# A fused slot-attention and FFN kernel: other places for an output block's mixed product, for low-part scalings and for queue steps

## The chip, the cores and the metric

The kernel runs as one program on one core of a Trainium2 chip. The metric is the time of one execution on the device, in microseconds (us). Each kernel is run several times and the median is given. One further execution is taken by the hardware profiler; its page and its trace are what this document reads. The engines are named as the profile names them: PE is TensorE's matrix products, PEld its weight loads, DVE is VectorE, ACT is ScalarE, POOL is GpSimd, SP is SyncE, which here only issues DMAs.

## The reference

The input is four token blocks of 512 tokens with 512 features (`hidden_states`, B = 4, T = D = 512). A layer norm without weights comes first, then an attention with gated slots, added to the input; then a second layer norm and a small FFN, added again.

```
q, k, v, s = split into 16 heads of xn @ Wq, @ Wk, @ Wv, @ Ws     # q, k: 64, v: 128, s: 64 slots
s = clip(s, -32, 32)
z = cumlogsumexp(s over t);  g_t = exp(z_{t-1} - z_t);  p_t = exp(s_t - z_t)
hk = hk * g_t + k_t p_t^T ;  ok_t = q_t hk          # first pass over the 64 slots
pv = softmax(ok)
hv = hv * g_t + p_t v_t^T ;  o_t = pv_t hv          # second pass
o  = o * rsqrt(mean(o^2) + eps) * g_norm * silu(xn @ Wg)
x  = x + o @ Wo
x  = x + (silu(xn2 @ fp8(gate_w) * scale) * (xn2 @ fp8(up_w) * scale)) @ fp8(down_w) * scale
```

All of it is in float32 from the outside. The recurrences over tokens are computed block by block.

## The kernel before, in words

Work is cut into 32 units. A unit is one group `g` of two heads (8 groups) for one token batch `b`. The units run in pairs of batches: for batches 0 and 1 the groups 0 to 7, each for both batches, in the order (0,0), (0,1), (1,0), (1,1), ... (7,1); then batches 2 and 3 in the same way. A unit is written (g,b). `first_unit` is (0,0), and `attention` (the function with most of the calls that the diff touches) writes all others. Unit (0,0) has no predecessor; every other unit also finishes the unit before it, which is called `before` in the code: it scales, transposes, splits and projects that unit's output while its own projections run. The last unit's output is finished inside the FFN.

A float32 product is made from three products of a shorter float type (`fp32r`): an operand is split into a high part, a low part and a part `less` that mixes both. The main product takes two passes (8 matmuls of 512 columns for a projection of the tokens), the mixed product one pass (4 matmuls). ACT copies the main product from PSUM with a factor, DVE then subtracts the mixed product. In `project_output` (L842) the inner dimension is only two heads, so the main product `p` has 4 matmuls and the mixed product `m` has 2. There are four such blocks `n` in a unit, one for each 128 tokens: p0, m0, p1, m1, p2, m2, p3, m3. ACT's copy `y` is L860, DVE's subtraction is L865 (`add_output`), and L866 adds the block to the residual stream in device memory by a DMA of POOL.

PSUM has three pools. `ps3` with tag `proj` has 3 buffers; all projections and both products of `project_output` rotate in it. `ps2` with tag `acc` has 2 buffers (the scores `a` and the outputs `ov`). `ps1` has three single banks that `bank()` hands out in turn: for transposes, for the states between blocks, and for the masked products `b`. A buffer is given again only when the last reader of its former content is done.

In order, a unit does: the slot scores `s`, keys `k`, queries `q` (each main and mixed), transposes of e and k; in even groups the values `v` of four token blocks (for two groups together); the transposes of the former unit's output (`turn_output`), its high part (`high_output`, ACT), low part and `less` (`split_output`, DVE, L832 to L836) and the scaling of the low part (`low_output`, ACT, L840); the products q times k with the mask; the gate `g` (`gate_main` twice and `gate_mixed`, copies on ACT at L519, main products at L514 and mixed ones at L537); the read of the slots (`ok`, `okn`), the softmax; then the output blocks 0 to 3, between them the transposes of the weights `w`; then `weight_slot`: the products `b` (L604), masked on DVE (L608); then `read_out`: the output `ov` by L765 and L774. The products at L774 wait for the masks.

The order on every engine is written by hand: the program has no scheduler (`tc.manual_schedule`). What goes on beside the units is held in two lists. `steps` holds the transposes of a coming layer norm; `next_step()` takes one. `work` holds small pieces on ACT, DVE, SP and POOL: scaling and splitting of weights (in `load_matrix`: `high` on ACT at L255, `rest` on DVE at L262 and L267, then a fetch and, at the end, a store of the split weights by SP), parts of layer norms (`measure`, `normalise` at L347, `parts` at L369 and L371, `scale_low` on ACT), and, for batches 2 and 3, the rounding of the FFN's weights to fp8 (DVE work and load and store DMAs; three steps make one piece). `other()` takes `pace[0]` entries of `work`, `other(1)` one, `piece()` takes entries up to the first that does not end a name with "_", `need(name)` takes all up to a name. `small` is `other` or `piece`, by the unit. `load(name)` issues the DMA of a coming matrix. `turned()` is true while parts of a layer norm stand first in the queue: this is so around the turn to the next pair of batches and to the FFN, in (7,0), (7,1), (0,2), (7,2) and (7,3), and at the start.

Of the kernel before, what the change touches and what calls it, by code (L numbers as in the profile page):

```python
# [37 lines left out]
F32 = mybir.dt.float32  # L38
# [6 lines left out]
P = 128  # L45
# [4 lines left out]
def kernel(  # L50
# [20 lines left out]
    B, T, D = x.shape  # L71
# [22 lines left out]
    ps3 = ctx.enter_context(tc.tile_pool(name="ps3", bufs=3, space=bass.MemoryType.PSUM))  # L94
# [15 lines left out]
    def bank(name, n=None):  # L110
        if n is None:
            n = turn[0]
            turn[0] = (n + 1) % 3
        if n in held:
            held.pop(n)()
        return ps1.tile([P, 512], F32, tag=f"bank{n}", name=name)
# [46 lines left out]
    work = []  # L163

    pace = [1]

    def other(count=None):
        for _ in range(count or pace[0]):
            if work:
                work.pop(0)[1]()  # L170

    def piece():

        while work:
            name, run = work.pop(0)
            run()
            if not name.endswith("_"):
                break

    def need(key):  # L180

        while any(name == key for name, _ in work):
            other(1)
# [4 lines left out]
    for g in range(NG):  # L188
# [3 lines left out]
        for nm in names:  # L192
            n = g if nm != "v" else 0 if g == 0 else (g + 1) // 2
# [94 lines left out]
    def turned():  # L288

        return bool(work) and work[0][0][:3] == "xs_"  # L290

    def next_step():
        if steps:
            steps.pop(0)()
# [340 lines left out]
    class Heads:  # L635
# [203 lines left out]
            lo = self.oT[:, 1, h, :]  # L839
            nc.scalar.mul(lo, lo.bitcast(F32), 1.0 / DELTA)  # L840

        def project_output(self, n):  # L842

            name = f"ps_o_{self.u}_{n}"
            p = ps3.tile([P, D], F32, tag="proj", name=name)
            m = ps3.tile([P, D], F32, tag="proj", name=name + "_m")
            for dst, which in ((p, (0, 1)), (m, (2,))):
                for i in which:
                    for h in range(HG):
                        nc.tensor.matmul(  # L850
                            dst,
                            self.oT[:, i, h, n * P : (n + 1) * P],
                            wt["o"][:, i, h * D : (h + 1) * D],
                            start=(i == which[0] and h == 0),
                            stop=(i == which[-1] and h == HG - 1),
                        )
            if n == 0:
                self.y_all = one.tile([P, NT, D], F32, tag="y", name=f"y_{self.u}")
            y = self.y_all[:, n, :]
            nc.scalar.mul(y, p, 1.0 + DELTA)  # L860
            self.y[n] = y, m
# [6 lines left out]
    def exp_and_log():  # L868
        nc.scalar.preload_act_table_set("natural_log_exp_and_others")

    def first_unit():


        X = Heads(0, 0)

        def between():
            for nm in "skqv":
                load_matrix(nm, 0, True)
            for item in [item for item in work if item[0] in ("s_", "k_", "q_")]:
                work.remove(item)  # L880
                item[1]()
            X.values(0)

        parts = layernorm(0, 1, between=between)
        for _ in range(7):
            piece()
        transposing = layernorm(1, 1)
        X.values(1)
        work.extend(parts())
        load_matrix("g", 0, True)  # L890
        other(3)
        X.slots()
        other(1)
        X.keys(X.running_sum)
        other(2)
        X.queries(None)
        X.turn_e()
        X.turn_k()
        other(2)
        X.values(2)  # L900
        other(1)
        X.key_states()
        X.inverse()
        X.values(3)
        fetch()
        fetch()
        load_matrix("o", 0, True)
        other(1)
        transposing()
        next_step()  # L910
        other(2)
        X.query_key()
        next_step()
        other(3)
        X.gate_main(0)
        piece()
        X.slot_scores()
        X.value_states()
        next_step()
        next_step()  # L920
        X.softmax()
        X.softmax_exp()
        other(2)
        X.gate_main(1)
        X.slot_weights()
        X.gate_silu(0)
        X.gate_silu(1)
        exp_and_log()
        X.weight_slot()
        X.softmax_sum()  # L930
        need("xs_0")
        piece()
        X.read_out()
        return X

    def attention(g, b, before, load, gated):

        X = Heads(g, b)  # L940
        even = g % 2 == 0
        small = other if even or b > 1 or pace[0] > 1 else piece

        def output(n):
            before.project_output(n)
            before.add_output(n)

        def early_step():

            if not any(name.endswith("_m") for name, _ in work):  # L950
                next_step()

        need(f"xs_{b}")
        need("s")
        X.slots()
        load("s")
        if not even:
            early_step()
        before.scale_output()
        need("k")  # L960

        def running_sum():
            before.scale_other()
            X.running_sum()
            small()

        X.keys(running_sum)
        load("k")
        if not even:
            early_step()  # L970
        need("q")
        X.queries(other if even or turned() else None)
        load("q")
        X.turn_e()
        if even:
            X.turn_k()
            next_step()
            if turned():
                other(1)
            need("v")  # L980
            X.values(0)
            X.values(1)
            before.turn_output(0)
            before.high_output(0)
            before.turn_output(1)
            before.high_output(1)
            X.key_states()
            X.inverse()
            X.query_key()
            other()  # L990
            X.values(2)
            before.split_output(0)
            before.low_output(0)
            other()
            next_step()
            X.values(3)
            before.split_output(1)
            before.low_output(1)
            other()
            next_step()  # L1000
        else:
            before.turn_output(0)
            X.turn_k()
            before.turn_output(1)
            before.high_output(0)
            before.high_output(1)
            X.query_key()
            X.key_states()
            before.split_output(0)
            before.split_output(1)  # L1010
            X.inverse()
            if work and work[0][0] == "o":
                other()
        need("g")
        X.gate_main(0)
        if not even:
            before.low_output(0)
            before.low_output(1)
        X.gate_mixed(0)
        if even:  # L1020
            other()
            next_step()
        elif work and work[0][0] == "o":
            other()
        X.gate_main(1)
        X.gate_mixed(1)
        load("g")
        if even:
            load("v")
        gated()  # L1030
        X.gate_silu(0)
        X.gate_silu(1)
        exp_and_log()
        X.slot_scores()
        X.value_states()
        X.softmax()
        if not turned():
            small()
        need("o")
        before.project_output(0)  # L1040
        X.softmax_exp()
        before.add_output(0)
        before.project_output(1)
        X.slot_weights()
        before.add_output(1)
        X.softmax_sum()
        next_step()
        output(2)
        output(3)
        load("o")  # L1050
        X.weight_slot()
        small()
        if even or b > 1 or steps:
            other()
        next_step()
        X.read_out()
        return X

# [75 lines left out]
    with tc.manual_schedule(engines=EVERY):  # L1134
# [11 lines left out]
        before = first_unit()  # L1146
# [3 lines left out]
        for i, (g, b) in enumerate(units[1:], 1):  # L1150
# [14 lines left out]
            def gated():  # L1165

                pace[0] = 1 + (pace[0] > 1 and i > 1)
                if g == NG - 2 and b % 2 == 1:
                    transposing[:] = [layernorm(*((2, 1) if b == 1 else (0, 2)))]
                elif g == NG - 1 and b % 2 == 0:  # L1170
                    transposing[0]()
                elif (g, b) == (NG - 1, 1):
                    need("xs_2")
                    transposing[0] = layernorm(3, 1)
# [28 lines left out]
            before = attention(g, b, before, load, gated)  # L1203
# [90 lines left out]
```

## Time and profile before

| what | value |
|---|---|
| runs | 1487.44, 1487.84, 1492.19 us; median 1487.84 |
| profiled execution | 1491.24 us |
| its span | 1489.5 us |
| mean granted clock of TensorE | 0.996 |
| PE busy | 1448.1 us, 97% of the span |
| PEld busy | 1168.6 us, 78% |
| DVE busy | 1106.0 us, 74% |
| ACT busy | 714.0 us, 48% |
| POOL busy | 193.9 us, 13% |
| first matmul | 6.2 us after the start |

The profiled execution is one execution beside the runs, so sums over the trace are made against 1489.5 (or 1491.24), not against the median. PE's busy time includes the pipelining of matmuls, whose ends are modelled. A row such as "PE a <- DVE b: 4.3, 19, 0.2" in the chain of waits says that PE waited for DVE's result b before a, 4.3 us in total, 19 times, at most 0.2. In a timeline, a row has the start, the duration, the engine, the line of the kernel and the operation, and in brackets the idle time in front of it and what ended it.

### The profile page before, as it was taken

The numbers are of one execution on the slowest core, as the hardware profiler recorded it, in microseconds if no ns is written. First come the engines' busy times: TensorE is split into PE (matmuls) and PEld (weight loads), VectorE is DVE, ScalarE is ACT, GpSimd is POOL, SyncE is SP. The second block draws the span as 40 slices with busy tenths as digits, with TensorE's granted clock in tenths as the row PEclk, the third lists the DMA queues.
The fourth block names the chain that finished last, engine by engine and source line by source line (L and its number), as shares of the span: only waits on it lengthen the run. The fifth ranks groups of instructions, "written<-read, shape, count | busy, mean of one in ns | idle before, by whom it ended". The sixth has DMA issues, their size and how long they took to land.

```text
span 1489.5 us, 22990 instructions
## 1 busy us (share of the span) xinstructions
PE 1448.1 (97%) x9053; PEld 1168.6 (78%) x9053; DVE 1106.0 (74%) x1968; ACT 714.0 (48%) x1214; POOL 193.9 (13%) x204
## 2 busy tenths in 40 slices
PE   7899999999999999999999999999999999999998
PEld 3678878888788887777877788888887788888886
DVE  7778768876887788777888888898888874445333
ACT  4556555555555555454544454445444553222221
POOL 2011111111111111211111111111112111000000
PEclk9999999999999999999999999999999999999999
DMA  8365555565656464446545755665565562101000
GB/s 325 113 173 174 149 156 160 179 185 156 170 170 182 130 226 120 135 122 214 158 109 143 238 135 136 178 204 157 142 176 171 142 177 29 57 1 57 1 29 29
DMA packets 80716, 212.52 MB, mean 143 GB/s; under 512 B 6153, under 2 KB 34849, under 8 KB 75425
## 3 DMA queue, kind: packets, MB, share of 16 engines
q1 hardware_dynamic: 62080, 177.49, 32.4%
q0 software_dynamic: 18528, 33.58, 15.5%
q8 instruction: 71, 1.16, 0.3%
q14 instruction: 37, 0.30, 0.1%
HBM read 107.23 MB, written 108.00 MB: 144 GB/s over the span
## 4 chain that ended last, share of the span: by engine, by line
PE 77%; DVE 15%; ACT 4%; issue 3%; DMA 0%; SPq 0%; DVEq 0%
PE ps_o L850 9%; PE ps_fg L1065 6%; PE ps_g L514 6%; PE ps_fu L1065 5%; PE ps_v L573 5%; PE ps_ov L774 4%; PE ps_g_m L537 3%; PE ps_o_m L850 3%; PE ps_s L514 3%; PE ps_k L514 3%; PE ps_q L514 3%; PE ps_fd L1109 3%; PE ps_b L604 2%; PE ps_v_m L573 2%; PE ps_fe L1109 2%
## 5 line engine op out<-in xcount | busy, mean ns | idle before, releaser
L866 POOL DMA_DIRECT2D stream<-y x128 | 110.9, 872 | 811.0 <-DVE y L865 808.8
L850 PE MATMUL ps_o<-w_o,oT 128*128 128x512 f32 x512 | 148.0, 410 | 5.8 <-ACT y L860 4.3
L514 PE MATMUL ps_g<-xs,w_g 128*128 128x512 f32 x496 | 125.4, 395 | 0.4 <-DVE v L582 0.4
L860 ACT ACTIVATE y<-ps_o 128x512 f32<-128x512 f32 x128 | 76.6, 599 | 99.2 <-PE ps_o L850 97.2
L573 PE MATMUL ps_v<-w_v,xs 128*128 128x512 f32 x480 | 122.3, 397 | 0.0
L1086 DVE SCALAR_TENSOR_TENSOR h<-ps_fu,scol,act 128x512 f32<-128x512 f32 x48 | 36.0, 750 | 107.0 <-PE ps_fu L1065 105.7
L850 PEld LDWEIGHTS ps_o<-w_o,oT 128*128 128x128 f32 x512 | 89.0, 188 | 33.5 <-ACT y L860 12.5
L514 PEld LDWEIGHTS ps_g<-xs,w_g 128*128 128x128 f32 x496 | 91.6, 188 | 20.6 <-DVE v L582 0.8
L865 DVE TENSOR_TENSOR y<-y,ps_o_m 128x512 f32<-128x512 f32 x128 | 87.2, 682 | 20.9 <-ACT y L860 19.4
L573 PEld LDWEIGHTS ps_v<-w_v,xs 128*128 128x128 f32 x480 | 87.8, 188 | 18.9
L1065 PE MATMUL ps_fg<-xs,wf 128*128 128x512 f32 x384 | 96.5, 393 | 0.0
L1065 PE MATMUL ps_fu<-xs,wf 128*128 128x512 f32 x384 | 95.0, 389 | 0.0
L582 DVE TENSOR_TENSOR v<-v,ps_v_m 128x512 f32<-128x512 f32 x60 | 41.1, 685 | 65.9 <-PE ps_v_m L573 59.4
L840 ACT ACTIVATE oT<-oT 128x512 fp32r<-128x512 f32 x64 | 40.5, 633 | 92.9 <-DVE oT L834 91.9
L1065 PEld LDWEIGHTS ps_fu<-xs,wf 128*128 128x128 f32 x384 | 72.1, 188 | 15.2
L1065 PEld LDWEIGHTS ps_fg<-xs,wf 128*128 128x128 f32 x384 | 71.1, 188 | 14.5
L784 ACT ACTIVATE og<-ps_ov 128x512 f32<-128x512 f32 x64 | 38.1, 598 | 90.9 <-PE ps_ov L774 90.9
L850 PE MATMUL ps_o_m<-w_o,oT 128*128 128x512 f32 x256 | 79.7, 392 | 0.0
L789 POOL TENSOR_TENSOR rs<-rs,mhalf 128x8 f32<-128x8 f32 x32 | 58.8, 1839 | 154.1 <-DVE rs L786 129.9
L1092 ACT CAST both<-h 128x512 fp32r<-128x512 f32 x48 | 29.8, 621 | 95.9 <-DVE h L1086 95.9
L1083 ACT ACTIVATE act<-ps_fg,scol 128x512 f32<-128x512 f32 x48 | 33.0, 688 | 81.7 <-PE ps_fg L1065 81.7
L581 ACT ACTIVATE v<-ps_v 128x512 f32<-128x512 f32 x60 | 35.7, 595 | 73.3 <-PE ps_v L573 73.3
(166 smaller groups left out, 3260.6 us busy)
## 6 DMA issues: line engine op xcount, KB each, us to landing
stream<-y POOLq DMA_DIRECT2D x128, 256.0 KB, 5.6
split_v<-w_v SPq DMA_DIRECT2D x4, 3072.0 KB, 12.5
split_g<-w_g SPq DMA_DIRECT2D x8, 1536.0 KB, 7.3
split_o<-w_o SPq DMA_DIRECT2D x8, 1536.0 KB, 7.1
w_v<-split_v SPq DMA_DIRECT2D x4, 3072.0 KB, 15.0
w_g<-split_g SPq DMA_DIRECT2D x8, 1536.0 KB, 6.5
w_o<-split_o SPq DMA_DIRECT2D x8, 1536.0 KB, 9.3
rounded<-qw SPq DMA_DIRECT2D x36, 256.0 KB, 3.1
```

What stands on the lines that cost most here:

```text
L514: nc.tensor.matmul(self.p, products(self.nm, c, self.col0, i), xs[self.b][i][:, c, :], start=(i == 0 and c == 0), stop=(i == 1 and c == KC ...
L537: nc.tensor.matmul(self.m, products(self.nm, c, self.col0, 2), xs[self.b][2][:, c, :], start=(c == 0), stop=(c == KC - 1),)
L573: nc.tensor.matmul(dst, xs[b][i][:, c, n * P : (n + 1) * P], wt["v"][:, i, c * 2 * HV : (c + 1) * 2 * HV], start=(i == which[0] and c == 0 ...
L582: nc.vector.tensor_tensor(to, to, m, ALU.subtract)
L774: nc.tensor.matmul(po[h][:, n, :], self.bb[h][:, n, :], both_v[self.b][:, n, self.v0 + h * DV : self.v0 + (h + 1) * DV], start=False, stop ...
L789: nc.gpsimd.tensor_tensor(rs, rs, mhalf.rearrange("p (h n) -> p h n", h=HG), ALU.pow)
L850: nc.tensor.matmul(dst, self.oT[:, i, h, n * P : (n + 1) * P], wt["o"][:, i, h * D : (h + 1) * D], start=(i == which[0] and h == 0), stop= ...
L860: nc.scalar.mul(y, p, 1.0 + DELTA)
L865: nc.vector.tensor_tensor(y, y, m, ALU.subtract)
L866: nc.gpsimd.dma_start(stream[self.b][n * P : (n + 1) * P, :], y, accum_op=ALU.add)
L1065: nc.tensor.matmul(pp, w[:, c * P : (c + 1) * P], xs[b][k][:, c, :], start=(c == 0 and k == 0), stop=(c == KC - 1 and k == 1),)
L1109: nc.tensor.matmul(sums[n], parts[k][:, n * P : (n + 1) * P], fw[c][2], start=(c == 0 and k == 0), stop=(c == NFC - 1 and k == 1),)
```

## The change

The number of instructions stays the same on every engine; what changes is their order on DVE, ACT, POOL and SP, and the PSUM buffer of one product for each unit. TensorE's instructions stay in the same order.

1. The mixed product of output block 2 (`m2`) is written to one of the three single banks instead of a buffer of `ps3`; only inside `attention`.
2. The step of the queue, `small()`, that stood behind `weight_slot` stands between output blocks 2 and 3.
3. In even groups `low_output(0)` and `low_output(1)`, which stood behind their `split_output`, follow the gate's first main product, as they do in odd groups. Around `values(3)`, `next_step` and `other` swap places, and `split_output(1)` comes behind the second pair of them instead of ahead of it.
4. In `first_unit` one `piece()` behind `gate_main(0)` goes, one of two steps moves from ahead of `gate_main(1)` to behind `slot_weights`, and one `piece()` comes behind `softmax_sum`. In unit (0,1) (`first`), the running sum takes one step instead of two.
5. At the turns: `piece()` does not stop at `scale_low`; in odd groups a `scale_low` that stands first is taken behind `inverse()`; and, while parts of a layer norm stand first, one more step is taken ahead of `read_out`.

```diff
@@ piece()
             run()
-            if not name.endswith("_"):
+            if not name.endswith("_") and run is not scale_low:
                 break
@@ project_output
-        def project_output(self, n):
+        def project_output(self, n, in_bank=False):
             p = ps3.tile([P, D], F32, tag="proj", name=name)
-            m = ps3.tile([P, D], F32, tag="proj", name=name + "_m")
+            m = bank(name + "_m") if in_bank else ps3.tile([P, D], F32, tag="proj", name=name + "_m")
@@ first_unit()
         X.gate_main(0)
-        piece()
         X.slot_scores()
...
         X.softmax_exp()
-        other(2)
+        other(1)
         X.gate_main(1)
         X.slot_weights()
+        other(1)
         X.gate_silu(0)
...
         need("xs_0")
         piece()
+        piece()
         X.read_out()
@@ attention()
+        first = pace[0] > 1 and even and b == 1
         def output(n):
-            before.project_output(n)
+            before.project_output(n, n == 2)
             before.add_output(n)
...
             X.running_sum()
-            small()
+            if first:
+                other(1)
+            else:
+                small()
...  (even groups)
             before.split_output(0)
-            before.low_output(0)
+            next_step()
+            other()
+            X.values(3)
             other()
             next_step()
-            X.values(3)
             before.split_output(1)
-            before.low_output(1)
-            other()
-            next_step()
...  (odd groups)
             X.inverse()
+            if work and work[0][1] is scale_low:
+                other(1)
             if work and work[0][0] == "o":
                 other()
         need("g")
         X.gate_main(0)
-        if not even:
-            before.low_output(0)
-            before.low_output(1)
+        before.low_output(0)
+        before.low_output(1)
         X.gate_mixed(0)
...
         output(2)
+        small()
         output(3)
         load("o")
         X.weight_slot()
-        small()
         if even or b > 1 or steps:
             other()
         next_step()
+        if turned():
+            other(1)
         X.read_out()
```

## The prediction

> **What bounds it now.** I read the page's busy times, then the chain that ended last, then the waits of TensorE, then the timeline stage by stage.
>
> ```profile
> PE 1448.1 (97%) x9053; PEld 1168.6 (78%) x9053; DVE 1106.0 (74%) x1968; ACT 714.0 (48%) x1214; POOL 193.9 (13%) x204
> ...
> PE 77%; DVE 15%; ACT 4%; issue 3%; DMA 0%; SPq 0%; DVEq 0%
> ```
>
> TensorE sets the end: 97% busy, and of the span of 1489.5 us 41.4 have no matmul, 6.2 of them before the first one. The change keeps TensorE's instructions and their order, so only lateness of its inputs can change. The waits that PE shows:
>
> ```profile
> PEld ps_o L850 <- ACT y L860: 12.5, 19, 0.7
> ...
> PE ps_xn L354 <- DVE xn L347: 8.0, 3, 6.2
> ...
> PE ps_o L850 <- ACT y L860: 4.3, 19, 0.2
> PE ps_xn L354 <- DVE xs L369: 4.1, 2, 2.1
> PE ps_kn L590 <- DVE kT L541: 2.6, 3, 1.7
> PE ps_okn L590 <- DVE sv L631: 1.7, 1, 1.7
> ```
>
> Columns: total, times, longest. The weight-load rows are larger than the matmul rows (12.5 against 4.3), since modelled matmul ends fill short stalls. So I price a stall by the distance between the starts of the weight loads of successive products, against the same distance in a unit that does not stall.
>
> **Part 1: block 2's mixed product in a bank.** Blocks 2 and 3 in unit (1,0), from the timeline of weight loads (start, duration; the bracket is idle time and its releaser):
>
> ```profile
> 129.67 0.42 PEld L850 LDWEIGHTS ps_o_m<-w_o,oT 128*128 128x128 f32 x2
> 130.75 0.76 PEld L850 LDWEIGHTS ps_o<-w_o,oT 128*128 128x128 f32 x4 [0.66 <-ACT y L860]
> 131.56 0.42 PEld L850 LDWEIGHTS ps_o_m<-w_o,oT 128*128 128x128 f32 x2
> ```
>
> With three buffers, block 3's main product (130.75) takes the buffer of block 2's and waits for its copy (ACT's L860, 130.10 to 130.70). m2 to p3 is 130.75 - 129.67 = 1.08, where m0 to p1 takes 0.46. With m2 in a bank, whose last readers (states) ended long before, p3 takes m0's old buffer or y1's, free by then; p3 to m3 grows 0.80 to 0.92. Net 0.62 - 0.12 = 0.50 us in 19 units of this kind; where m2 to p3 is 0.83 or 0.78, 0.25. Sum if nothing else binds: about -12.
>
> **Part 2: the queue step between blocks 2 and 3.** DVE's timeline beside it:
>
> ```profile
> 131.25 0.68 DVE L865 TENSOR_TENSOR y<-y,ps_o_m 128x512 f32<-128x512 f32 x1
> 132.62 0.69 DVE L865 TENSOR_TENSOR y<-y,ps_o_m 128x512 f32<-128x512 f32 x1 [0.69 <-ACT y L860]
> 133.53 1.29 DVE L608 TENSOR_TENSOR b<-ps_b,tri 128x512 f32<-128x512 f32 x2 [0.23 <-PE ps_b L604]
> 134.73 0.68 DVE L262 TENSOR_TENSOR w_v<-raw_v,w_v 128x512 fp32r<-128x512 f32 x1
> ```
>
> The step (L262 and L267) stood behind the masks (L608); now it is ahead of y3's subtraction (the second L865) and both masks on DVE's queue, and `ps_ov`'s product waits for the masks. From y2's subtraction to the mask is 133.53 - 131.25 = 2.28 now (2.13 in the 0.83 units). Afterwards DVE needs y2, X, y3, about 1.2 + X: for a weight step X = 0.72 + 0.61 = 1.33, so 2.53; a first, second, third quantize step has X = 0.69, 1.05, 1.34. TensorE, with part 1, would allow 1.78 (1.88). The later of both, less the present distance, is the change for each unit:
> - weight step: 6 units x +0.25, 4 x +0.40
> - no step: 4 units x -0.25, 1 x -0.50
> - first quantize step: 4 x -0.39; second 3 x +0.14; third 5 x +0.26; two others +0.04
>
> Sum +1.8: DVE takes nearly all of the 12. A weight step also puts a 0.60 us scaling on ACT ahead of y3's copy; ACT idled 1.28 before this copy, so it hides, and if it did not, 0.6 in ten units. Its fetch or store, and the quantize DMAs, go on SP ahead of `load("o")`; on POOL, only y's stores (0.87 each, POOL 13% busy) shift. I see no DMA wait for these sources in the units concerned; so 0, at most one transfer of about 2.5 us (the longest such wait here, once) each. A step taken early frees DVE later: the transposes of k wait for kT in six units of batches 2 and 3 (loads e to kn 0.97, 1.25, 1.27, 0.98, 0.62, 0.62, against 0.56). Bounds 0 and -2.35; I take -1.8.
>
> **Part 3: low parts behind the gate's copy.** ACT's timeline in unit (2,0):
>
> ```profile
> 190.42 0.63 ACT L840 ACTIVATE oT<-oT 128x512 fp32r<-128x512 f32 x1 [3.43 <-DVE oT L834]
> 190.95 0.58 ACT L581 ACTIVATE v<-ps_v 128x512 f32<-128x512 f32 x1
> 193.62 0.63 ACT L840 ACTIVATE oT<-oT 128x512 fp32r<-128x512 f32 x1 [2.08 <-DVE oT L834]
> 194.15 1.15 ACT L519 ACTIVATE sg<-ps_g 128x512 f32<-128x512 f32 x2
> ```
>
> ACT stands 2.08 us in front of L840 for DVE's L834, and the gate's copies of finished products wait behind it (they run as one group, 194.15), holding buffers: `ps_g_m`'s load at 194.78 has 0.60 of idle, ended by sg. Behind the copy, low parts find L834 done, and the second gate's copy has 2.56 us to spare before its buffer is wanted. Excess of the gate's distances over 1.81, 0.91, 1.81, 1.22: 0.56 in five even units, 0.35 in three, 0.13 in three, 0.04 in two, together -4.3; in (0,1), -1.93. With the swap around `values(3)` the second `other` stands ahead of `split_output(1)` on DVE; its output is wanted only behind the gates, at the first low scaling's place plus 0.6, and by then DVE has caught up.
>
> **Part 4: the first units.** From the waits above: okn 1.72 at 49.69 in (0,0), b 0.89 at 55.08 (DVE's wT), and kn 1.73 of the 2.6, at 69.80 in (0,1). Two of the gate's weight pieces (1.33 of DVE each) leave DVE's queue ahead of `sv` and `wT`. With them taken out of the queue, `sv` is there when PE arrives (okn at 48.0, -1.7), wT too, and block b then waits for L369 of the fourth token block, done at 53.95 by the same durations: -1.1. The pieces come back behind the softmax sum, ahead of the reductions of (0,0)'s squares and of eT and kT in (0,1): those end 0.6 and 0.5 later than they could, and kT, ahead of which the running sum now takes one step of the queue instead of two, is ready at 67.5; kn starts at 68.2 instead of 69.80: -1.6. Bounds 0 and -4.3 (the three waits together).
>
> **Part 5: the turn to the next batch.** Unit (7,0):
>
> ```profile
> 574.24 0.83 PE L354 MATMUL ps_xn<-ident,xn 128*128 128x128 f32 x4 [2.06 <-DVE xs L369]
> 575.00 1.65 PE L765 MATMUL ps_ov<-sv,wT 64*128 64x128 f32 x12
> 576.58 2.68 PE L774 MATMUL ps_ov<-v,b 128*128 128x128 f32 x16
> ```
>
> L369 (573.41 + 0.68) stands behind the masks and releases the bank. Afterwards the queue's two steps there stand ahead of y3 and the masks: DVE has y2 until 571.35, L369 to 572.0, its twin L371 to 572.7, the next normalise (0.54) to 573.3, y3 to 573.9, the first mask to 574.6. The blocks b, one of whose banks L369 frees, begin at 570.5 and wait until 572.0 (1.4 of idle, for 2.06), and `ps_ov` follows at 574.9 for 576.58: -1.7. The clock row decides how much more:
>
> ```profile
> 574.66:578.06 3.40, 3.40 (x21) 2.84 (x21) 1.91 (x4) 0.60 (x1) 0.00 (x0) 0.52 0.82 123
> ```
>
> After the window's ends and length come the engines' busy times; the last value but two is the granted clock: 0.52 for 3.4 us, behind an idle of 2.06. It costs 0.63 in `ps_ov` (2.68 against 2.05), 0.23 in the transposes, 0.8 in the products after them: 1.7. The Trainium skill ("TensorE: Matmul & The Clock Gate", section "What's actually happening") has half clock only after at least one idle window of about 3.4 us; by that, a 2.06 us gap would not halve anything, and the gain here would be the stall alone. The row disagrees, in both turns ((7,2) too: 0.52 over 1172 to 1175.4), while gaps of 1.44 to 1.73 cost no clock. I take the row: s_7_1 loads at 576.7 instead of 579.0, -2.3; (7,2) by the same steps 1173.5 instead of 1176.5, -3.0, its L369 being ready earlier. By the rule the two would give 3.4 less. Unit (7,1): the wait of 1.47 on w_o's L262 and the slow loads behind it go, -2.03, less 0.2 that the pieces delay `okT`: -1.85. Unit (0,2): the transposes waiting for the fourth normalise (part of the first row of waits, 1.44, with the distance to `g_m` 2.71 against 0.91) go, since that step comes earlier: -1.6. Sum -8.75. The POOL power and the SP load that swap places with single DMAs have nothing waiting.
>
> **Sum.** -1.6 (first) -1.9 (unit (0,1)) -4.3 (low parts) +1.8 (parts 1 and 2) -1.8 (kT) -8.75 (turns) = -16.6 us. The profiled execution took 1491.2 with a span of 1489.5; its span becomes 1472.9 and it 1474.6. The median of the runs shown, 1487.8, is 3.4 under it, so 1471.
>
> **Rivals.**
> - A: the masks have slack that the weight-load distances hide, so part 1's 12 us come through: another 13.6, 1458. For it: `ps_ov` (L774, 134.27) shows only 0.30 of waiting for the mask. Against: by then DVE has no idle left. Chance 0.13.
> - B: as worked out: 1471; 0.55, its own range 1465 to 1478.
> - C: the turns become new waits (b waits for L369 as long as the transposes did, and the half clock stays), and the first units and kT give nothing: 8.75 + 1.6 + 1.8 = 12.2 lost, 1483. For it: a late L369 only changes who waits for it. Against: it is 1.4 earlier. 0.20, of which 0.08 is counted as within the 0.3%.
> - D, slower: the step taken 2.5 to 3 us earlier meets a source that has not landed; then DVE's L262 (or ACT's scaling before y3's copy) stands, and y3, masks and `ps_ov` behind it. It decides from (16.6 + 4.5) / 26 = 0.8 us in each of 26 units; there it gives 1488 + 4.5 = 1492. For it: nothing between blocks 2 and 3 has slack left on DVE. Against: L262 now starts without a DMA wait, and raw weights are fetched units ahead. 0.11; 0.01 is left for what I name nowhere.
>
> **The numbers.** This kernel's measurement tells 0.3%, 4.5 us. Faster: 0.55 + 0.13 + 0.12 of C = 0.80; same 0.08 + 0.01 = 0.09; slower 0.11. Range: from A, 1458, to just past C, 1484; outside lie D and what A might add.
>
> **What would show it.** Part 1: the wait of p3 for y's copy, 12.5, gone. Part 2: a wait of `ps_ov` for the masks that grows from 0.30 to 0.7 or more in weight units, and L262 between two L865. Part 3: `ps_g_m` waiting for sg gone. Part 4: okn without its 1.72. Part 5: no 0.5 clock around 575 and 1172, and `ps_b` waiting for L369. Wrong if ACT or DVE shows DMA waits in front of L255 or L262, or if `ps_ov` waits by more than 1 us in most units.

## The result, and the profile after

The changed kernel takes 1470.26 us (median of four runs, 1468.81 to 1471.32), the kernel before 1488.55 (four runs, 1487.44 to 1492.19). The ratio is 0.9872, 95% interval 0.9853 to 0.9892: faster by 1.3%. Its profiled execution took 1470.09 with a span of 1468.4, against 1491.24 and 1489.5. So the two profiles differ by 21.1 us and the medians by 18.3; why they do is taken up under "The offset".

The names in the rows: eT and kT are the slot scores and the keys as DVE leaves them, e and kn their transposes, okn that of the read of the slots, oT the transposes and parts of the former unit's output, sg the gate, y an output block. The page of the changed kernel has the same count of instructions on PE and 17.9 us less of busy time (short stalls count as busy where modelled ends fill them); the time without a matmul falls from 41.4 to 38.2:

```profile
PE 1430.2 (97%) x9053; PEld 1170.6 (80%) x9053; DVE 1104.3 (75%) x1968; ACT 714.5 (49%) x1214; POOL 194.0 (13%) x204
...
PE 85%; DVE 11%; issue 2%; ACT 1%; DMA 0%; SPq 0%; DVEq 0%
```

The chain that ended last goes through PE for 85% of the span, 77% before. The waits of its matmuls (total, times, longest):

```profile
PE ps_ov L774 <- DVE b L608: 14.8, 24, 0.9
PE ps_xn L354 <- DVE xn L347: 6.5, 2, 6.1
PE ps_b L604 <- DVE xs L369: 3.1, 3, 1.5
...
PE ps_kn L590 <- DVE kT L541: 0.8, 1, 0.8
PE ps_q L514 <- DVE eT L541: 0.6, 1, 0.6
```

The waits of `ps_o` for y's copy, of `ps_xn` for L369, of okn for sv and of `ps_g_m` for the gate's copy are gone. Four took a place: `ps_ov` for the masks, absent from the matmul rows before and now the largest of all; `ps_b` for L369; `ps_q` for eT; and okn for its copy of DVE (0.5, once, in (7,1)).

Unit (1,0) again, first the weight loads, then DVE:

```profile
125.78 0.42 PEld L850 LDWEIGHTS ps_o_m<-w_o,oT 128*128 128x128 f32 x2
126.24 0.88 PEld L850 LDWEIGHTS ps_o<-w_o,oT 128*128 128x128 f32 x4
127.16 0.42 PEld L850 LDWEIGHTS ps_o_m<-w_o,oT 128*128 128x128 f32 x2
127.94 0.97 PEld L604 LDWEIGHTS ps_b<-wT,eT 64*128 64x128 f32 x16 [0.35 <-issue]
128.82 0.75 PEld L765 LDWEIGHTS ps_ov<-sv,wT 64*128 64x128 f32 x12
130.62 0.52 PEld L774 LDWEIGHTS ps_ov<-v,b 128*128 128x128 f32 x4 [1.04 <-DVE b L608]
```

```profile
127.36 0.68 DVE L865 TENSOR_TENSOR y<-y,ps_o_m 128x512 f32<-128x512 f32 x1
127.95 0.68 DVE L262 TENSOR_TENSOR w_v<-raw_v,w_v 128x512 fp32r<-128x512 f32 x1
128.67 0.69 DVE L267 SCALAR_TENSOR_TENSOR w_v<-w_v 128x512 fp32r<-128x512 f32 x1
129.28 0.68 DVE L865 TENSOR_TENSOR y<-y,ps_o_m 128x512 f32<-128x512 f32 x1
129.88 1.28 DVE L608 TENSOR_TENSOR b<-ps_b,tri 128x512 f32<-128x512 f32 x2
```

From m2 to p3 is 126.24 - 125.78 = 0.46, the stall is gone. But L262 and L267 now stand between the two L865, DVE runs from 127.36 to the masks without a break, and the mask starts 129.88 - 127.36 = 2.52 behind y2's subtraction, as forecast (2.53). PE has its blocks b ready in time and waits 1.04 at 130.62, where it waited 0.30.

ACT in unit (2,0), and PE and the granted clock (the last value but two of the window's row) in unit (7,0):

```profile
188.45 0.60 ACT L519 ACTIVATE sg<-ps_g 128x512 f32<-128x512 f32 x1 [2.17 <-PE ps_g L514]
188.95 1.14 ACT L840 ACTIVATE oT<-oT 128x512 fp32r<-128x512 f32 x2
...
191.18 0.60 ACT L519 ACTIVATE sg<-ps_g 128x512 f32<-128x512 f32 x1 [1.09 <-PE ps_g L514]
```

```profile
565.12 0.49 PE L604 MATMUL ps_b<-wT,eT 64*128 64x128 f32 x2
566.78 1.13 PE L604 MATMUL ps_b<-wT,eT 64*128 64x128 f32 x14 [1.18 <-DVE xs L369]
567.84 0.66 PE L354 MATMUL ps_xn<-ident,xn 128*128 128x128 f32 x4
568.42 0.94 PE L765 MATMUL ps_ov<-sv,wT 64*128 64x128 f32 x12
569.29 2.05 PE L774 MATMUL ps_ov<-v,b 128*128 128x128 f32 x16
```

```profile
566.50:570.00 3.50, 3.22 (x36) 2.84 (x37) 3.46 (x7) 1.11 (x2) 1.56 (x2) 1.00 0.99 135
```

Each gate copy now waits for PE and not behind a scaling. In (7,0) the blocks b wait 1.18, in place of 2.06 at the transposes, and the clock stays whole: `ps_ov` takes 2.05 instead of 2.68.

### The profile page after: what moved, and what is told of

Its sections match the earlier page's. It is cut to its first block, busy times and chain, and to the rows that moved or that the text cites. A ratio compares the mean times of both kernels' runs of the same rounds, so it can differ in the third digit from the quotient of the medians.

```text
span 1468.4 us, 23007 instructions
## 1 busy us (share of the span) xinstructions
PE 1430.2 (97%) x9053; PEld 1170.6 (80%) x9053; DVE 1104.3 (75%) x1968; ACT 714.5 (49%) x1214; POOL 194.0 (13%) x204
## 4 chain that ended last, share of the span: by engine, by line
PE 85%; DVE 11%; issue 2%; ACT 1%; DMA 0%; SPq 0%; DVEq 0%
PE ps_g L514 8%; PE ps_v L573 8%; PE ps_fg L1071 6%; PE ps_fu L1071 6%; PE ps_o L850 5%; PE ps_ov L774 4%; PE ps_s L514 4%; PE ps_g_m L537 4%; PE ps_v_m L573 4%; PE ps_q L514 4%; PE ps_k L514 4%; DVE y L865 3%; PE ps_fd L1115 3%; PE ps_fe L1115 2%; PE ps_o_m L850 2%; PE ps_a L604 2%
## 5 line engine op out<-in xcount | busy, mean ns | idle before, releaser
L850 PE MATMUL ps_o<-w_o,oT 128*128 128x512 f32 x512 | 144.2, 403 | 0.0
L865 DVE TENSOR_TENSOR y<-y,ps_o_m 128x512 f32<-128x512 f32 x128 | 87.2, 681 | 2.1 <-ACT y L860 1.2
L774 PE MATMUL ps_ov<-v,b 128*128 128x128 f32 x512 | 65.7, 281 | 15.4 <-DVE b L608 14.8
L774 PEld LDWEIGHTS ps_ov<-v,b 128*128 128x128 f32 x512 | 59.6, 191 | 21.4 <-DVE b L608 21.1
```

The costliest lines, as they stand in the source:

```text
L774: nc.tensor.matmul(po[h][:, n, :], self.bb[h][:, n, :], both_v[self.b][:, n, self.v0 + h * DV : self.v0 + (h + 1) * DV], start=False, stop ...
L850: nc.tensor.matmul(dst, self.oT[:, i, h, n * P : (n + 1) * P], wt["o"][:, i, h * D : (h + 1) * D], start=(i == which[0] and h == 0), stop= ...
L865: nc.vector.tensor_tensor(y, y, m, ALU.subtract)
```

## The experiments

Where a term is compared by units, it is by the distances between the starts of weight loads, unit by unit, against the same distances of the other kernel.

**Part 1 alone.** In the kernel before, only this:

```diff
-            before.project_output(n)
+            before.project_output(n, n == 2)
```

> The kernel before with part 1 alone: block 2's mixed product in a bank, the queue step still behind weight_slot. Theory (the early step on DVE is what used up part 1's gain in the changed kernel): the distance from m2 to p3 falls to 0.46 and p3 to m3 grows to 0.93 in every unit, nothing is inserted on DVE ahead of the masks, so 0.49 us in 19 units and 0.24 in 12 come through: about 12 us, 1476, a little more if the bank taken for m2 also pulls L369 forward in (7,0) and (7,2). Rival (the masks or the ov product had no slack anyway): the distance falls, but the wait of ov for the mask grows by the same, 1485 to 1488.

Measured 1475.66 us (1474.12 to 1478.23), ratio 0.9906 (0.9889 to 0.9922). The loads of block 2's mixed product, of p3 and m3 in (1,0):

```profile
128.43 0.42 PEld L850 LDWEIGHTS ps_o_m<-w_o,oT 128*128 128x128 f32 x2
128.89 0.88 PEld L850 LDWEIGHTS ps_o<-w_o,oT 128*128 128x128 f32 x4
129.81 0.42 PEld L850 LDWEIGHTS ps_o_m<-w_o,oT 128*128 128x128 f32 x2
```

Every unit with the longer stall gains 0.45 to 0.54 (the last, (7,3), 0.37), every other 0.22 to 0.28, and nothing is given back at `ps_ov`: 11.3 us outside the turns. In (7,0) and (7,2) it gains 2.0 and 2.5, more than the stall: taking a bank for m2 pulls out the layer-norm part that holds it, so L369 is ahead of the masks. The idle moves to the blocks b (1.77 and 1.23), and no half clock follows it, which is 1.5 of the gain in each. Apart from the clock, part 1 is worth its 12 us as long as nothing stands between blocks 2 and 3 on DVE.

**The changed kernel with the step behind again.**

```diff
         output(2)
-        small()
+        ahead = turned()
+        if ahead:
+            small()
         output(3)
         load("o")
         X.weight_slot()
+        if not ahead:
+            small()
```

> The changed kernel with the queue step back behind weight_slot, except where parts of a layer norm stand first in the queue. Theory: ov no longer waits for the masks (0.6 to 0.75 us in 10 weight units, 0.6 in 5 units and 0.3 in 3 units with quantize steps, about 11 us), but the transposes of k wait for kT again (2.2 us in batches 2 and 3, 1.5 in (1,1), (3,1), (5,1)): about 8 us under the changed kernel, 1462. Rival (the step's place does not matter once the bank is there): 1470. Rival (the late step costs more than the early one): over 1472.

Measured 1461.18 us (1459.85 to 1461.76), ratio to the kernel before 0.9801 (0.9787 to 0.9816), so 9 us under the changed kernel's median. The distance in front of L774 falls from 1.79 to 1.05 in the weight units and from 1.66 or 1.39 to 1.05 in the quantize units; kn waits for kT again, 0.4 to 0.7 in four units of batches 2 and 3. The other wait that comes back, 0.5 in each of three units, is not the one expected: it is in (1,0), (3,0) and (5,0), behind kn, where the next transposes wait for ACT's copy of e. By distances it is 8.7 us, the start of (0,0) aside. The early step thus cost the changed kernel some 9 us net: the masks had no slack.

**The changed kernel without part 1.**

```diff
-            before.project_output(n, n == 2)
+            before.project_output(n)
```

> The changed kernel without part 1: m2 in the buffers of the projections again. Theory: in units whose early step is long (weight steps, third quantize steps) DVE sets the masks in both cases, and nothing changes; only the units without a step (4 of 0.25, one of 0.5) and with a first quantize step (4 of 0.43) lose: about 3 us, 1473 to 1474. Rival (the parts add up independently): 12 us more, 1482.

Measured 1473.29 us (1472.85 to 1474.16), ratio to before 0.9885 (0.987 to 0.9899): 3.0 above the changed kernel's median. In six of the weight units m2 to p3 is 1.08 again, a net 0.5, and the distance in front of L774 shrinks by as much (1.79 to 1.29); in the other four both change by 0.26. Their sums agree to 0.04. Outside the first unit and the turns, only units without a step (0.25 and 0.5), with a first quantize step (0.40 to 0.45) and (6,3) (0.2) lose. So the same edit is worth 12 us by itself and 3 beside the early step: both wait for the same masks, and only the later counts.

**Part 3 alone.**

```diff
             before.split_output(0)
-            before.low_output(0)
+            next_step()
             other()
+            X.values(3)
+            other()
             next_step()
-            X.values(3)
             before.split_output(1)
-            before.low_output(1)
-            other()
-            next_step()
...
         X.gate_main(0)
-        if not even:
-            before.low_output(0)
-            before.low_output(1)
+        before.low_output(0)
+        before.low_output(1)
```

> The kernel before with part 3 alone: the low parts scaled behind the gate's copy in even groups, with the swap of steps around the values. Theory: the gate's distances become 1.81, 0.91, 1.81, 1.1 in all even units: 2.0 in (0,1) and 4.3 in the others, 6.3 in all, 1482. Rival (ACT catches up anyway, or the wait moves to the softmax): 1487 to 1489.

Measured 1483.04 us (1482.51 to 1483.35), ratio 0.9949 (0.9934 to 0.9964). The gate's distances become 1.81, 0.91, 1.81, 1.22 in every even unit, within 0.07: 1.9 less in (0,1) and 4.3 in the others, as forecast (4.6 by their whole units). There is one gain more: in (0,2) the distance from `g_m` to the transposes behind it falls from 2.71 to 0.92, and the unit by 1.66 us. That stall, which I had given to part 5, goes by part 3's swap of steps around `values(3)`: in (0,2), DVE's L369, L371 and L347 now fill an idle of 1.67 us that stood ahead of them.

**Part 4 alone.** The diff of `first_unit` and `first`, in the kernel before.

> The kernel before with part 4 alone (the steps of the first two units). Theory: okn's wait of 1.72 and wT's wait go, block b waits about 1.5 for L369 in their place, kn's wait of 1.73 goes but the keys' mixed product waits about 1 for eT: 1.0 us less up to the gates of (0,1), nothing elsewhere, about 1 us in the span. Rival (the full sum of the three waits): 4.3 us. Rival (all of it given back): nothing.

Measured 1486.83 us in one run, which is no time for an effect of this size; the distances tell: 1.05 less in (0,0) at okn and b, and in (0,1) 0.66 less up to the kn transposes (the keys wait 0.46 for eT, then kn 1.12 less), and 0.8 at the gate of (0,1). Elsewhere nothing, within 0.06, but for the very start of (0,0), which differs from profile to profile (see part 5). That is 2.5: less than the full sum, more than the 1.0 expected.

**Part 5 alone**, with the step between blocks 2 and 3 only while parts of a layer norm stand first:

```diff
-            if not name.endswith("_"):
+            if not name.endswith("_") and run is not scale_low:
...
             X.inverse()
+            if work and work[0][1] is scale_low:
+                other(1)
...
         next_step()
+        if turned():
+            other(1)
         X.read_out()
```

> The kernel before with part 5 alone: scale_low does not end a piece and is taken in odd groups, the queue step stands between blocks 2 and 3 only where parts of a layer norm stand first, and one more step stands ahead of read_out there. Theory: the idle of 2.06 us in (7,0) and (7,2) goes and with it the half clock, (7,1) loses its wait for w_o: 2.5, 1.9 and 3.2 us, 7.6 in all; mean granted clock 0.999 or 1.0; the wait of 1.44 in (0,2) stays, since part 3's swap of steps removed it. Rival (the wait only moves to b): 2 us or less, and a clock of 0.996 to 0.998.

Measured 1477.53 us (1476.73 to 1478.67), ratio 0.9916 (0.99 to 0.9932), clock 1.0 in the profile: 2.8 in (7,0), 2.0 in (7,1), 3.7 in (7,2), nothing in (0,2). Not expected was (0,1): 3.2 us less, 2.0 of them at kn, whose distance falls from 2.55 to 0.56. A `piece()` that does not end at `scale_low` takes one weight piece of the gate with it, and the pieces behind it move up. DVE around kT in (0,1), with part 5 alone:

```profile
61.30 1.23 DVE L670 TENSOR_TENSOR_SCAN z<-eT 128x512 f32<-128x512 f32 x1
62.44 0.67 DVE L262 TENSOR_TENSOR w_o<-raw_o,w_o 128x512 fp32r<-128x512 f32 x1
63.14 0.69 DVE L267 SCALAR_TENSOR_TENSOR w_o<-w_o 128x512 fp32r<-128x512 f32 x1
63.75 0.68 DVE L541 TENSOR_TENSOR kT<-kT,ps_k_m 128x512 f32<-128x512 f32 x1
```

and in the kernel before:

```profile
65.64 0.67 DVE L262 TENSOR_TENSOR w_o<-raw_o,w_o 128x512 fp32r<-128x512 f32 x1
...
67.72 0.69 DVE L262 TENSOR_TENSOR w_o<-raw_o,w_o 128x512 fp32r<-128x512 f32 x1 [0.69 <-ACT w_o L255]
...
69.06 0.68 DVE L541 TENSOR_TENSOR kT<-kT,ps_k_m 128x512 f32<-128x512 f32 x1
```

One weight piece stands between the scan and kT, where the kernel before had two. Of the 13.3 us between the medians, turns and (0,1) hold 11.7; one unit, (4,0), is 0.35 longer. The start of (0,0) is 3.0 shorter in this profile, which is no part of the change. The first eight value products, in the kernel before and here:

```profile
9.69 6.18 PE L562 MATMUL ps_v<-raw_v,xn_whole 128*128 128x512 f32 x8 [0.92 <-DMA raw_v<-in_L_attn_Wv_dram]
```

```profile
8.82 4.08 PE L562 MATMUL ps_v<-raw_v,xn_whole 128*128 128x512 f32 x8
```

Of the 3.0, 1.1 is an earlier landing of their weights and 1.9 is the clock. In the kernel before the loads of these products stand 0.86 apart up to 14.1, and the trace has the clock whole from 14.74 on; here it is whole from 9.80 on, and the loads stand 0.43 apart. How long the start was in the other executions is open.

**Part 2 alone**, without the turns:

```diff
         output(2)
+        ahead = not turned()
+        if ahead:
+            small()
         output(3)
...
         X.weight_slot()
-        small()
+        if not ahead:
+            small()
```

> The kernel before with part 2 alone: the queue step between blocks 2 and 3, except where parts of a layer norm stand first. Theory: ov waits longer for the masks in 10 weight units (0.25 to 0.4) and 8 quantize units (about 0.1), 4 us in all, and the transposes of k wait less for kT (2.2 in batches 2 and 3, 1.5 in (1,1), (3,1), (5,1)): the two cancel, within 1 us of the kernel before. Rival (the early step is pure loss): 4 us slower. Rival (it is a gain by itself): 4 us faster.

Measured 1488.80 us (1488.0 to 1489.23, twelve runs) beside 1490.81 of the kernel before (fifteen runs); ratio 0.9992 (0.9983 to 1.0001), no difference that can be told. The waits of all weight loads of `ps_ov`, in the kernel before:

```profile
PEld ps_ov L774 <- DVE b L608: 8.9, 30, 0.3
```

and with part 2 alone:

```profile
PEld ps_ov L774 <- DVE b L608: 12.9, 30, 0.7
```

The masks cost 4.0 more. The waits of kn for kT in batches 2 and 3 return 2.2 and those for ACT's copy of e in (1,0), (3,0) and (5,0) 1.5: outside the turns and the start of (0,0) the distances sum to zero within 1 us. The early step is no gain by itself.

**The running sum's step behind the keys**, beyond the change, on top of the kernel with the late step:

```diff
+        later = []
         X.keys(running_sum)     # running_sum: later.append(small), but for (0,1) and the turns
+        for step in later:
+            step()
```

> A kernel beyond the change: the changed kernel with the queue step back behind weight_slot (except at the turns), and with the queue step of the running sum moved behind the keys' mixed product, so that kT's subtraction no longer stands behind it on DVE. Theory: the waits of kn for kT that came back with the late step (3.2 us of PE's loads, 3.7 by the distances between loads) go, and qT is wanted late enough: 1457 to 1458. Rival (DVE is then late for qT or for the outputs' transposes): 1461 or more.

Measured 1460.39 us (1459.05 to 1460.95), ratio to before 0.9799 (0.9783 to 0.9815). In four units of batches 2 and 3 the wait for kT goes (2.1 us, e to kn 0.56 again); in (1,0), (3,0) and (5,0) the transposes behind kn still start 1.0 after it. In (1,0):

```profile
109.21 0.66 DVE L541 TENSOR_TENSOR kT<-kT,ps_k_m 128x512 f32<-128x512 f32 x1
...
110.65 0.62 ACT L255 ACTIVATE w_v<-raw_v 128x512 fp32r<-128x512 f32 x1
...
111.17 0.58 ACT L519 ACTIVATE qT<-ps_q 128x512 f32<-128x512 f32 x1
111.23 0.47 PEld L590 LDWEIGHTS ps_kn<-ident,kT 128*128 128x128 f32 x4
...
111.64 0.57 ACT L682 COPY e<-ps_e 128x512 f32<-128x512 f32 x1
...
112.27 0.42 PEld L590 LDWEIGHTS ps_oT<-ident,og 128*128 128x128 f32 x4 [0.57 <-ACT e L682]
```

kT is done at 109.87, long before kn loads. The next transposes wait for ACT's copy of e, and ACT, which has no idle here, has a scaling of w_v (L255) and the copy of qT ahead of it. The place of DVE's step could not remove this wait. Against the late-step kernel's median it is 0.8 less, where 3 to 4 was expected; the profile has a start of 1.1 us more, around the first values, which hides part of it.

**The changed kernel without part 4.**

```diff
-            if first:
-                other(1)
-            else:
-                small()
+            small()
...  (and first_unit as before)
```

> The changed kernel without part 4 (the steps of the first two units as before), with parts 1, 2, 3 and 5. Theory: piece() of part 5, which no longer stops at scale_low, already brings the gate's weight pieces forward, so kT is in time in (0,1) without part 4; okn's wait of 1.72 comes back (distance sum of (0,0) up by 1.06), but the keys' mixed product no longer waits for eT (0.98) and kn no longer for kT (1.1): the span falls by about 1 us, 1469. Rival (part 4 is what removes kn's wait): 2 to 3 us slower, 1472 to 1473.

Measured 1469.78 us (1469.14 to 1470.63), ratio to before 0.9865 (0.9847 to 0.9883), which can't be told from 1470.26. By distances: (0,0) 1.06 more, (0,1) 2.05 less (the keys no longer wait for eT, 0.98, nor kn for kT, 1.09). (7,1) and (4,2) are 0.4 longer each, though DVE has the same instructions there; it idles 0.28 once in front of each mask. The rest is equal. So beside part 5, part 4 costs 1.0 in the first two units; the whole time of this kernel does not show it, the distances of the next one do. That the pieces which part 4 puts behind the softmax sum are the ones that `piece()` would have taken earlier is my reading of the code, not shown.

**All of these together**: both late steps (behind `weight_slot` and behind the keys), no part 4, and

```diff
-            before.project_output(n, n == 2)
+            before.project_output(n, n == 2 and not turned())
```

> A kernel beyond the change: steps behind weight_slot and behind the keys' mixed product (as in the two kernels before it), without part 4, and with m2 in a bank except where parts of a layer norm stand first. Theory: 1.0 less from the first units and 0.6 less from the turns, where the bank taken for m2 makes b wait for L369: 1458.8. Rival (these waits were hidden): 1460.4.

Measured 1458.58 us (1458.17 to 1459.21), ratio to before 0.979 (0.9775 to 0.9805). It is the fastest of all, 11.7 under the changed kernel's median. By distances, leaving out part 4 gives its 1.0; the exception for m2 gives 0.2 in (7,0) and 0.3 in (7,2) and loses 0.3 in (0,2), so that 0.2 is left of the 0.6 expected. The waits that PE has left (the third row is that of (1,0), (3,0) and (5,0)):

```profile
PE ps_xn L354 <- DVE xn L347: 6.5, 2, 6.2
PE ps_okn L590 <- DVE sv L631: 1.7, 1, 1.7
PE ps_oT L590 <- ACT e L682: 1.0, 3, 0.3
PE ps_b L604 <- DVE wT L751: 0.9, 1, 0.9
PE ps_ov L774 <- DVE b L608: 0.8, 1, 0.8
```

**The kernel before again**, for the clock; nothing is edited.

> The kernel before once more, profiled and timed, for the clock. Theory: the clock is set by windows of 3.41 us that follow each other without a break, and an idle of 2.06 us halves it only when one window holds all of it (60%); so some executions have both halved stretches (span about 1489 to 1490, clock 0.996), some one or none (1486 to 1487, 0.998), and the profile shows the one or the other with the same two idles of 2.06. Rival (such an idle always halves): spans within 0.5 us of each other and the same clock in every run.

Measured 1489.68 us over twelve runs, with spans from 1486.5 at a mean clock of 0.999 to 1491.1 at 0.996. PE and the granted clock in the two turns of its profile:

```profile
573.78 1.09 PE L354 MATMUL ps_xn<-ident,xn 128*128 128x128 f32 x4 [2.06 <-DVE xs L369]
...
1171.36 0.63 PE L354 MATMUL ps_xn<-ident,xn 128*128 128x128 f32 x4 [2.06 <-DVE xs L369]
```

```profile
573.85:577.25 3.40, 3.40 (x20) 2.85 (x21) 2.26 (x4) 0.60 (x1) 0.00 (x0) 0.52 0.81 133
1171.40:1174.80 3.40, 3.40 (x33) 3.11 (x34) 2.52 (x6) 1.18 (x2) 0.00 (x0) 1.00 1.01 310
```

The same idle of 2.06 us, and the clock is halved behind the first and whole behind the second. In the first profile of this kernel it was halved behind both; there the two halved stretches begin 597.3 us apart, 175 times 3.413. Counted from this profile's first halved stretch, which begins at 573.71, in the same steps, a window edge falls at 1171.04 and cuts the idle into 1.74 and 0.32; in (7,0) one window holds 2.0 of it. With part 2 alone it is the other way round: the edge cuts the first idle (0.8 and 1.26; clock whole), the second lies in one window (clock halved). The rival falls: such an idle doesn't always halve. The count holds across the second idle too: behind the last matmuls of this profile the clock falls to half at 1485.07, which is 911.36 us after 573.71, 267 of the same steps.

## Why the prediction was right or wrong

The forecast was 1471 and the result 1470.26, by likeliest case B. That it came so near is in part luck: the sum against the profile was 4.5 us too small, and an offset of 3.4 to the median, which the changed kernel does not have, made up for most of it. By steps, in us:

| step | predicted | by distances of loads |
|---|---|---|
| start of (0,0), clock whole from 12.94 instead of 14.74 on | none | -0.9 (no part of the change) |
| part 4 with kn in (0,1) | -1.6 | -0.9 |
| low parts, (0,1) | -1.9 | -2.0 |
| low parts, other even units | -4.3 | -4.6 |
| transposes in (0,2) | -1.6 | -1.6 |
| parts 1 and 2, `ps_ov` | +1.8 | +0.9 |
| kT in batches 2 and 3 | -1.8 | -2.2 |
| transposes behind kn in (1,0), (3,0), (5,0) | none | -1.5 |
| turns (7,0), (7,1), (7,2) | -7.15 | -7.8 |
| sum | -16.6 | -20.6 |

**Right.** Parts 1 and 2: of some 12 us of stalls, DVE takes all, as worked out (weight units +0.25 and +0.41, no step -0.25 and -0.49, first quantize step -0.4). The first two experiments show this from both sides, and the third that part 1 is worth 3 us beside part 2. Rival A's slack does not exist. Part 3 held in each class of units. The turns went from a wait of L369 behind the masks to a shorter one ahead of them, with no half clock; rival C had the new wait right, and its size wrong. Rival D did not come: in the changed kernel, DVE's L262 between blocks 2 and 3 did not wait for a source in any of the ten weight units, and DVE ran without a break in front of their masks.

**Off in size.** A third quantize step costs 0.1 in a unit, not 0.26: X was right, the mask stands 2.52 to 2.53 behind y2's subtraction, but I compared it with the 2.28 of unit (1,0), and in these five units it was 2.41 to 2.43 before. The kT waits came back in full (2.2 for 1.8). The step "a step taken early frees DVE later" was applied to batches 2 and 3 alone. It gains in (1,0), (3,0) and (5,0) too, where the transposes behind kn started 1.02 after it, against 0.51 in the other odd units, a difference in the trace that I had passed over and then, in what I expected of the experiments, put in the wrong units and down to kT.

**Wrong in cause.** The step "Unit (0,2) ... go, since that step comes earlier" stood under the turns; part 3 alone removes this wait, part 5 alone does not. And part 4's term holds for part 4 alone, where kn comes 1.7 earlier (1.05 and 0.66). Beside part 5 it does not: part 5's `piece()` brings kT in time by itself, and part 4 then costs 1.0. What failed is the step "kn starts at 68.2 instead of 69.80: -1.6": it priced part 4 without part 5 and costed eT's lateness at 0.5, where in the changed kernel the keys' next product loses 0.98 and kn still waits 0.8; -0.9 is left.

**The offset.** "The median of the runs shown is 3.4 under it, so 1471" carries the profile's excess over to the changed kernel, which has none: its profiled execution, 1470.09, lies at its median. Part of the excess is the two half-clock stretches, which not every execution has (the one profiled again, with one stretch, took 1489.42); the change takes them away, so I counted that gain twice. Part is the few runs: 49 later executions of the kernel before have a median of 1489.93, only 1.3 under the profiled one. And part is a long start: the transposes behind the first values load at 15.27 in this profile, and between 12.32 and 15.97 in all thirteen. How much each holds is open. The false offset stood in for the terms that I had missed.

**The clock rule.** The Trainium skill ("TensorE: Matmul & The Clock Gate", section "What's actually happening") says that the window is free-running, and that half clock follows an idle window of about 3.4 us. The first half agrees with the two starts 175 windows apart, and the stretches last 3.41; the second asks for too much: 1.97 to 2.06 us of idle within one window were enough here, in eight idles of five profiles; 1.74 were not. I had taken the row as what a gap of 2.06 always does, which is as wrong; it does so in those executions in which nearly all of the gap falls into one window.

## What to carry to other kernels

A stall removed on one engine is worth only the distance to the next engine that reaches the same product late: before moving work ahead of that product, sum the queue of every engine in front of it, for both edits together. An edit of queue places should be tried with each other edit taken out, since here one was worth 12 us alone and 3 in company, and another, by distances, gained 2.5 alone and lost 1.0 in company. Before a wait is put down to an input, look which product stands idle and what ended its idle time: a distance that starts at one product can belong to the next one. Take a profiled execution's excess over the median as something to explain, not as a constant to carry over.

## What the runs showed of the hardware

TensorE's clock fell to half for 3.41 us behind eight of ten idles of 2.06 us, and not behind idles of 1.44 to 1.77 in the profiles here. In the two that cost nothing, a window edge left at most 1.74 and 1.26 us in one window. The same program had such stretches in some executions and not in others, since the windows' phase differs. The spans of the kernel before go with the clock (1486.1 to 1486.6 us at a mean of 0.999, 1488.6 to 1491.1 at 0.996), but at 0.998 alone they reach from 1485.9 to 1490.3, so this mean is not all that spreads them. It leaves out the start, where products run at half pace until the clock becomes whole: at 14.74 us in the profile of the kernel before, at 9.80 with part 5 alone, at 15.52 with the keys first, and the first eight value products took 6.18, 4.08 and 6.26 us. The changed kernel, without long idles, has a clock of 0.999 or 1.0 in every run.
